# Pairwise outer products with batch normalisation: a rearranged head, and long rows stored in halves with the shortest rows on VectorE

## The chip, the cores and the metric

One core of a Trainium2 chip. The metric is device time in microseconds (us) of one execution; "median" is over the runs of one kernel. All runs told here had the full TensorE clock (granted clock 1.0). Runs of one kernel agree within about 0.7 us, so differences of half a microsecond can be read where a run was repeated five times. The experiments ran in four rounds on four chips; the kernel before, run in each, had medians of 1891.0 to 1891.2 us, so a comparison across rounds carries up to 0.2 us more.

Engines are called PE (TensorE), DVE (VectorE), ACT (ScalarE), POOL (GpSimd) and SP (SyncE, which issues the stores) in the profile.

## The reference

For 1024 samples, 39 fields and 16 components, every pair (row r > column c) gives a 16 x 16 outer product, which is normalised over the batch per pair and weighted:

```python
cross  = xj[:, rows, :, None] * xi[:, cols, None, :]        # (1024, 741, 16, 16)
mean   = jnp.mean(cross, axis=(0, 2, 3), keepdims=True)
var    = jnp.mean(jnp.square(cross - mean), axis=(0, 2, 3), keepdims=True)
normed = (cross - mean) * jax.lax.rsqrt(var + BN_EPS)
normed = normed * gamma[None, :, None, None] + beta[None, :, None, None]
out    = normed[:, :, None, :, :] * W[None, None, :, :, :]  # 777 MB
```

Mean and variance of all 741 pairs follow from small 39 x 39 matrices of moments, so the statistics cost some 30 us; from then on the kernel makes and stores 777 MB.

## The kernel before

A *tile* is one row r (r pairs) of T = 2 of each partition's 8 samples; a tile of a row from 20 to 37 shares one of two slots of a big SBUF buffer with the same samples of the short row 38 - r, which comes right after it. A tile's life:

```python
xs = scale_xi(n)        # POOL: xi * s, s = gamma * rstd per pair
products(n)             # per sample and component i: xs * xj[r, i]; most i on ACT, 4 or 5 of 16 on POOL
finish(n)               # (product + t) * w; DVE one pair of both samples at a time, POOL the row's last 13%
store(n, c0, c1)        # SP: pairs c0..c1; the last piece of a row over 24 is stored sample by sample
```

```python
ONE, TWO = 24, 31
    def bounds(n):
        if n < len(FIRST_PIECES):
            return FIRST_PIECES[n]
        r = tiles[n][0]
        pieces = 1 + (r > ONE) + (r > TWO)          # halves over 24, thirds over 31
        return tuple(q * r // pieces for q in range(pieces + 1))
...
        for n in range(2 * NT // T):                # the head: moments
            square(n)
            emit(raw0, 2)                           # products of tile 0, unscaled, between the squares
            moments(n)
...
        emit(raw_products(1, nc.gpsimd, range(8, 32)), 24)   # tile 1, unscaled too
        emit(raw0, 8)
        nc.scalar.copy(g1, ps_g[0][0:F, 0 : 2 * F + 1])      # the table chain starts here
...
        apply(0)                                    # DVE: gamma and beta into the table of one group of rows
        affine(0)                                   # tiles 0 and 1: scale and shift afterwards
        weigh(0)                                    # DVE: * w, piece by piece, and store
        scale_xi(2)
        affine(1)
        weigh(1)
```

## Time and profile before

| | |
|---|---|
| median | 1891.2 us (1891.1 to 1891.6, 6 runs) |
| output | 777 MB, 414 GB/s over the span |
| first store issued | 41.3 us |
| DVE, ACT, POOL busy | 92, 86, 83% |
| DMA busy | 90% or more in 39 of 40 slices |

One line of the page: the number of packets, each one contiguous run of a partition's row.

```profile
DMA packets 70288, 783.67 MB, mean 415 GB/s; under 512 B 5057, under 2 KB 6209, under 8 KB 15937
```

### The profile page before, as it was taken

The numbers are of one execution on the slowest core, as the hardware profiler recorded it, in microseconds if no ns is written. First come the engines' busy times: TensorE is split into PE (matmuls) and PEld (weight loads), VectorE is DVE, ScalarE is ACT, GpSimd is POOL, SyncE is SP. The second block draws the span as 40 slices with busy tenths as digits, with TensorE's granted clock in tenths as the row PEclk, the third lists the DMA queues.
The fourth block names the chain that finished last, engine by engine and source line by source line (L and its number), as shares of the span: only waits on it lengthen the run. The fifth ranks groups of instructions, "written<-read, shape, count | busy, mean of one in ns | idle before, by whom it ended". The sixth has DMA issues, their size and how long they took to land. (4 is left out here: it accounts for less than half of the span.)

```text
span 1889.3 us, 10288 instructions
## 1 busy us (share of the span) xinstructions
PE 24.5 (1%) x128; PEld 23.1 (1%) x128; DVE 1730.7 (92%) x2612; ACT 1621.3 (86%) x3625; POOL 1574.5 (83%) x1985
## 2 busy tenths in 40 slices
PE   3100000000000000000000000000000000000000
PEld 3100000000000000000000000000000000000000
DVE  7999999998989898989898989899999999999996
ACT  8999989898989898989898989888888888888762
POOL 9798878788888888888888888888888888888972
DMA  4999999999999999999999999999999999999999
GB/s 164 390 418 429 425 427 429 430 424 429 424 425 426 424 424 426 422 425 425 424 425 423 426 423 426 422 422 422 421 421 422 418 415 419 416 419 419 415 419 390
DMA packets 70288, 783.67 MB, mean 415 GB/s; under 512 B 5057, under 2 KB 6209, under 8 KB 15937
## 3 DMA queue, kind: packets, MB, share of 16 engines
q1 hardware_dynamic: 69632, 780.46, 98.3%
q10 hardware_dynamic: 576, 2.56, 0.3%
q14 instruction: 79, 0.64, 0.1%
q8 instruction: 1, 0.02, 0.0%
HBM read 6.00 MB, written 776.99 MB: 414 GB/s over the span
## 5 line engine op out<-in xcount | busy, mean ns | idle before, releaser
L238 DVE SCALAR_TENSOR_TENSOR y_sb<-y_sb,st_sb,w_dve 128x512 f32<-128x512 f32 x2542 | 1678.5, 740 | 131.5 <-issue 128.3
L139 ACT ACTIVATE y_sb<-xs,xj_sb 128x256 f32<-128x256 f32 (+32 forms) x3544 | 1576.4, 539 | 223.5 <-DMA out_dram<-y_sb 171.8
L141 POOL TENSOR_SCALAR y_sb<-xs,xj_sb 128x560 f32<-128x560 f32 (+35 forms) x1256 | 643.2, 536 | 35.1 <-DMA out_dram<-y_sb 32.6
L230 POOL TENSOR_TENSOR y_sb<-y_sb,w_sb 128x1024 f32<-128x1024 f32 (+4 forms) x138 | 442.0, 3203 | 11.5
L159 POOL TENSOR_TENSOR xs<-xi_sb,st_sb 128x576 f32<-128x576 f32 (+37 forms) x150 | 187.8, 1252 | 225.3 <-ACT y_sb L139 217.8
L226 POOL TENSOR_SCALAR y_sb<-y_sb,st_sb 128x512 f32<-128x512 f32 x384 | 259.4, 692 | 12.9 <-ACT y_sb L139 12.9
L204 DVE TENSOR_TENSOR y_sb<-y_sb,w_dve 128x2560 f32<-128x2560 f32 (+5 forms) x8 | 21.0, 2682 | 2.3 <-ACT y_sb L194 2.3
L139 ACT ACTIVATE y_sb<-xi_sb,xj_sb 128x304 f32<-128x304 f32 x40 | 18.7, 534 | 0.1
L414 PE MATMUL ps<-y_sb 39*128 39x38 f32 (+37 forms) x76 | 16.5, 397 | 5.6 <-DVE y_sb L402 5.6
L414 PEld LDWEIGHTS ps<-y_sb 39*128 39x128 f32 x76 | 16.3, 329 | 5.8 <-issue 5.8
L194 ACT ACTIVATE y_sb<-y_sb,st_sb 128x512 f32<-128x512 f32 x20 | 14.2, 797 | 0.0
L196 POOL TENSOR_SCALAR y_sb<-y_sb,st_sb 128x512 f32<-128x512 f32 x18 | 13.5, 771 | 0.3 <-issue 0.3
L141 POOL TENSOR_SCALAR y_sb<-xi_sb,xj_sb 128x304 f32<-128x304 f32 x24 | 11.9, 518 | 0.0
L299 DVE TENSOR_REDUCE y_sb<-y_sb 128x78 f32<-128x1248 f32 x8 | 11.1, 1442 | 0.0
L277 DVE TENSOR_REDUCE y_sb<-xj_sb 128x78 f32<-128x1248 f32 (+1 forms) x5 | 5.9, 1189 | 5.6 <-DMA xj_sb<-in_r_xj_dram 5.6
L293 ACT ACTIVATE y_sb<-y_sb 128x1248 f32<-128x1248 f32 x8 | 9.9, 1243 | 1.3 <-POOL y_sb L283 1.1
L283 POOL TENSOR_TENSOR y_sb<-xj_sb,y_sb 128x1248 f32<-128x1248 f32 x4 | 9.3, 2314 | 1.9 <-ACT y_sb L327 1.9
L283 POOL TENSOR_TENSOR y_sb<-xi_sb,y_sb 128x1248 f32<-128x1248 f32 x4 | 9.3, 2318 | 0.0
L316 PE MATMUL ps<-y_sb 128*39 128x79 f32 x48 | 7.2, 339 | 16.5 <-DVE y_sb L299 16.5
L316 PEld LDWEIGHTS ps<-y_sb 128*39 128x39 f32 x48 | 6.1, 183 | 17.4 <-DVE y_sb L299 9.6
L277 DVE TENSOR_REDUCE y_sb<-xi_sb 128x78 f32<-128x1248 f32 (+1 forms) x5 | 5.9, 1186 | 0.0
L259 POOL TENSOR_SCALAR_AFFINE_SELECT y_sb<-y_sb 39x4992 f32<-39x4992 f32 x1 | 4.6, 4623 | 0.0
(45 smaller groups left out, 16.9 us busy)
## 6 DMA issues: line engine op xcount, KB each, us to landing
out_dram<-y_sb SPq DMA_DIRECT2D x32, 3072.0 KB, 13.7
out_dram<-y_sb SPq DMA_DIRECT2D x28, 2816.0 KB, 15.7
out_dram<-y_sb SPq DMA_DIRECT2D x32, 1664.0 KB, 14.2
out_dram<-y_sb SPq DMA_DIRECT2D x16, 3328.0 KB, 17.2
out_dram<-y_sb SPq DMA_DIRECT2D x30, 1536.0 KB, 15.2
out_dram<-y_sb SPq DMA_DIRECT2D x12, 3840.0 KB, 17.6
out_dram<-y_sb SPq DMA_DIRECT2D x12, 3584.0 KB, 18.1
out_dram<-y_sb SPq DMA_DIRECT2D x22, 1792.0 KB, 17.4
```

What stands on the lines that cost most here:

```text
L139: nc.scalar.activation(y, src, AF.Copy, scale=scale)
L141: engine.tensor_scalar(y, src, scale, 1.0, ALU.mult, ALU.mult)
L159: nc.gpsimd.tensor_tensor(xs, xi_sb[:, t0 : t0 + T, 0:r, :], s_sb[:, :, n0 : n0 + r, :].to_broadcast([P, T, r, E]), ALU.mult,)
L194: nc.scalar.activation(y[:, :, c, :], y[:, :, c, :], AF.Identity, bias=t_c, scale=s_c)
L196: nc.gpsimd.tensor_scalar(y[:, :, c, :], y[:, :, c, :], s_c, t_c, ALU.mult, ALU.add)
L204: nc.vector.tensor_tensor(y[:, :, c0:c1, :], y[:, :, c0:c1, :], w_dve.unsqueeze(1).to_broadcast([P, T, c1 - c0, EE]), ALU.mult,)
L226: nc.gpsimd.tensor_scalar(y[:, :, c, :], y[:, :, c, :], t_sb[:, n0 + c : n0 + c + 1], 1.0, ALU.add, ALU.mult)
L230: nc.gpsimd.tensor_tensor(y[:, :, split:r, :], y[:, :, split:r, :], w_sb.unsqueeze(1).to_broadcast([P, T, r - split, EE]), ALU.mult,)
L238: stt(y[:, :, c, :], y[:, :, c, :], t_sb[:, n0 + c : n0 + c + 1], w_dve.to_broadcast([P, T, EE]), ALU.add, ALU.mult,)
L283: nc.gpsimd.tensor_tensor(devs[n % 7], sources[x][:, t0 : t0 + T], shift[:, x : x + 1, :].unsqueeze(3).to_broadcast([P, T, F, E]), ALU.sub ...
L316: nc.tensor.matmul(acc[0:F, 0 : 2 * F + 1], lhs, fb[:, t], start=t == 0, stop=t == NT - 1)
L414: nc.tensor.matmul(ps[:, :, first[r] - n0 : first[r] - n0 + r], pick[:, r, :], stq[:, :, 0:r], start=True, stop=True,)
```

## The change

Its intent is to send the first store off earlier and to give the late rows larger pieces without starving the stores. The core of the diff, with cuts marked:

```diff
-ONE, TWO = 24, 31
+ONE, LONG = 24, 33
-POOL_I, POOL_I_LONG = 4, 5
+POOL_I, POOL_I_LONG, POOL_I_FIRST = 4, 5, 6      # POOL_I_LONG now for rows over 33, not over 31
+POOL_SHARE, POOL_PAIRS_LONG = 0.13, 8
+SHORT = 4
 ... # head: loads sample by sample, xi before xj, the first xi in two halves;
 ... # the Gram products of x = 1 and x = 0 apart; the square of the table chain on DVE
-        raw1 = raw_products(1, nc.scalar, range(8))          # tile 1 no more prepared before the table
 ...
         apply(0)
-        affine(0)
-        weigh(0)
-        scale_xi(2)
-        affine(1)
-        weigh(1)
-        apply(2)
-        apply(1)
+        apply(1)
+        affine(0, range(0, 11))
+        scale_xi(1)
+        affine(0, range(11, mid))
+        nc.scalar.copy(xj_short, xj_sb[:, :, 1 : SHORT + 1, :])   # for the short rows, in PSUM
+        weigh(0)
+        products(1)                                               # finished sample by sample
 ...
-        pieces = 1 + (r > ONE) + (r > TWO)
+        pieces = 1 + (r > ONE)                                    # halves for all rows over 24
 ...
+        if r <= SHORT:                     # products of rows of up to 4 pairs: three DVE operations
+            nc.vector.tensor_tensor(xs, xi, s_short)              # (arguments cut)
+            for t in range(T):
+                nc.vector.tensor_tensor(view(n)[:, t], xs[:, t], xj_short)
 ...
+        long = r > LONG                    # eight pairs at the end of the first half:
+        for c in range(c0, c1):            # ACT adds t, POOL multiplies by w, in two steps of four
+            nc.scalar.activation(y[:, :, c, :], y[:, :, c, :], AF.Identity, bias=t_c)
+        nc.gpsimd.tensor_tensor(y[:, :, c0:c1, :], y[:, :, c0:c1, :], w_sb, ALU.mult)
```

More of the change, by code (lines that the diff above doesn't have):

```diff
@@ L15 @@
 T = 2
-ONE, TWO = 24, 31
+ONE, LONG = 24, 33
 FIRST_PIECES = (
-    (0, 2, 5, 9, 14, 19), (0, 6, 12, 19), (0, 4, 11, 19), (0, 9, 19), (0, 10, 20), (0, 9, 18), (0, 10, 20), (0, 9, 18)
+    (0, 2, 5, 9, 14, 19), (0, 4, 9, 14, 19), (0, 4, 11, 19), (0, 9, 19), (0, 10, 20), (0, 9, 18), (0, 10, 20), (0, 9, 18)
 )
-POOL_I, POOL_I_LONG = 4, 5
-POOL_SHARE = 0.13
-LOADS = (0, 1, 2, 4, 8)
+POOL_I, POOL_I_LONG, POOL_I_FIRST = 4, 5, 6
+POOL_SHARE, POOL_PAIRS_LONG = 0.13, 8
+LOADS = (1, 2, 3, 4, 8)
+SHORT = 4
 ROW_GROUPS = (
-    (19, 20, 0, None), (15, 19, 1, None), (20, 25, 1, None), (1, 15, 2, 8), (25, 32, 3, 16), (32, 39, 4, 24)
+    (19, 20, 0, None), (15, 19, 1, None), (20, 25, 2, 1), (1, 15, 2, 8), (25, 32, 3, 16), (32, 39, 4, 24)
 )
@@ L71, in tile_pair_outer_batchnorm @@
             slot ^= 1
-    RAW = 2
+    RAW = 1
     cpool = ctx.enter_context(tc.tile_pool(name="cpool", bufs=1))
+    scaled_short = ctx.enter_context(tc.tile_pool(name="scaled_short", bufs=1))
     scaled = ctx.enter_context(tc.tile_pool(name="scaled", bufs=2))
@@ L124, in tile_pair_outer_batchnorm @@
     ps_s, ps_c, ps_g = banks[0], banks[1], banks[2:5]
+    xj_short = ps_c.rearrange("p (t r i) -> p t r i", t=NT, i=E)
     ps_st = banks[5:7] + ps_g
@@ L156, in scale_xi @@
         r, t0, _ = tiles[n]
+        if r <= SHORT:
+            return
         n0 = first[r]
@@ L167, in products @@
     def products(n):
+        r, t0, _ = tiles[n]
+        if r <= SHORT:
+            xs = scaled_short.tile([P, T, r, E], F32, tag="xs_short", name=f"xs_{r}_{t0}")
+            nc.vector.tensor_tensor(
+                xs,
+                xi_sb[:, t0 : t0 + T, 0:r, :],
+                s_short[:, first[r] : first[r] + r]
+                .unsqueeze(1)
+                .unsqueeze(3)
+                .to_broadcast([P, T, r, E]),
+                ALU.mult,
+            )
+            for t in range(T):
+                nc.vector.tensor_tensor(
+                    view(n)[:, t].rearrange("p n (i j) -> p n i j", j=E),
+                    xs[:, t].unsqueeze(2).to_broadcast([P, r, E, E]),
+                    xj_short[:, t0 + t, r - 1 : r, :].unsqueeze(3).to_broadcast([P, r, E, E]),
+                    ALU.mult,
+                )
+            return
         xs = xs_of.pop(n)
-        split = E - (POOL_I_LONG if tiles[n][0] > TWO else POOL_I)
+        split = E - (POOL_I_FIRST if n < 3 else POOL_I_LONG if tiles[n][0] > LONG else POOL_I)
         for t in range(T):
@@ L173, in products, with store @@
                 product(n, nc.scalar if i < split else nc.gpsimd, t, i, xs[:, t])
-    def store(n, c0, c1):
+    def store(n, c0, c1, t_from=0, t_to=T):
         r, t0, _ = tiles[n]
         n0 = first[r]
-        step = 1 if r > ONE and c1 == r else T
-        for t in range(0, T, step):
+        step = 1 if r > ONE and c1 == r else t_to - t_from
+        for t in range(t_from, t_to, step):
             nc.sync.dma_start(
@@ L184, in store, with affine @@
             )
-    def affine(n):
+    def affine(n, pairs):
         r = tiles[n][0]
         y = view(n)
-        for c in range(r):
+        for c in pairs:
             s_c = st_sb[:, 0, first[r] + c : first[r] + c + 1]
@@ L223, in finish @@
         y = view(n)
-        split = r - int(r * POOL_SHARE + 0.5)
-        for c in range(split, r):
-            nc.gpsimd.tensor_scalar(
-                y[:, :, c, :], y[:, :, c, :], t_sb[:, n0 + c : n0 + c + 1], 1.0, ALU.add, ALU.mult
-            )
-        if split < r:
+        long = r > LONG
+        p1 = r // 2 if long else r
+        p0 = p1 - (POOL_PAIRS_LONG if long else int(r * POOL_SHARE + 0.5) if r > SHORT else 0)
+        step = POOL_PAIRS_LONG // 2 if long else r
+        for c0 in range(p0, p1, step):
+            c1 = min(c0 + step, p1)
+            for c in range(c0, c1):
+                t_c = t_sb[:, n0 + c : n0 + c + 1]
+                if long:
+                    nc.scalar.activation(y[:, :, c, :], y[:, :, c, :], AF.Identity, bias=t_c)
+                else:
+                    nc.gpsimd.tensor_scalar(
+                        y[:, :, c, :], y[:, :, c, :], t_c, 1.0, ALU.add, ALU.mult
+                    )
@@ L230, in finish @@
             nc.gpsimd.tensor_tensor(
-                y[:, :, split:r, :],
-                y[:, :, split:r, :],
-                w_sb.unsqueeze(1).to_broadcast([P, T, r - split, EE]),
+                y[:, :, c0:c1, :],
+                y[:, :, c0:c1, :],
+                w_sb.unsqueeze(1).to_broadcast([P, T, c1 - c0, EE]),
                 ALU.mult,
             )
-        for c0, c1 in zip(bounds(n), bounds(n)[1:]):
-            for c in range(c0, min(c1, split)):
-                stt(
-                    y[:, :, c, :],
-                    y[:, :, c, :],
-                    t_sb[:, n0 + c : n0 + c + 1],
-                    w_dve.to_broadcast([P, T, EE]),
-                    ALU.add,
-                    ALU.mult,
-                )
-            store(n, c0, c1)
+        size = 1 if n == RAW else T
@@ new lines, in finish @@
+        for t in range(0, T, size):
+            for c0, c1 in zip(bounds(n), bounds(n)[1:]):
+                for c in [*range(c0, min(c1, p0)), *range(max(c0, p1), c1)]:
+                    stt(
+                        y[:, t : t + size, c, :],
+                        y[:, t : t + size, c, :],
+                        t_sb[:, n0 + c : n0 + c + 1],
+                        w_dve.to_broadcast([P, size, EE]),
+                        ALU.add,
+                        ALU.mult,
+                    )
+                store(n, c0, c1, t, t + size)
@@ L248, in tile_pair_outer_batchnorm @@
     with tc.manual_schedule():
+        nc.gpsimd.memset(ones, 1.0)
+        nc.sync.dma_start(xi_sb[:, 0, 0 : F // 2], xi_v[:, 0, 0 : F // 2])
+        nc.scalar.dma_start(xi_sb[:, 0, F // 2 : F], xi_v[:, 0, F // 2 : F])
+        nc.sync.dma_start(xj_sb[:, 0], xj_v[:, 0])
         for t0, t1 in zip(LOADS, LOADS[1:]):
+            if t1 == NT:
+                nc.scalar.activation(shift_r, ones[0:F, 0:1], AF.Sqrt)
             nc.sync.dma_start(xj_sb[:, t0:t1], xj_v[:, t0:t1])
@@ L255, in tile_pair_outer_batchnorm @@
         nc.sync.dma_start(w_sb[:, 0, :], w.rearrange("o i j -> (o i j)").partition_broadcast(P))
-        nc.gpsimd.memset(ones, 1.0)
         nc.gpsimd.memset(fb[:, :, 2 * F : 2 * F + 1], 1.0 / NB)
@@ L273, in part, with sums @@
             return slice(x * F, (x + 1) * F)
-        def sums(t0, t1):
-            for x in range(2):
+        def sums(t0, t1, xs=(1, 0)):
+            for x in xs:
                 nc.vector.tensor_reduce(
@@ L279, in sums, with step_of @@
                 )
+        def step_of(n):
+            return n // 2 * T, 1 - n % 2
         def deviation(n):
-            t0, x = n // 2 * T, n % 2
+            t0, x = step_of(n)
             nc.gpsimd.tensor_tensor(
@@ L290, in square @@
         def square(n):
-            scale = 0.25 / NB**0.5 if n % 2 else 0.25
+            _, x = step_of(n)
+            scale = 0.25 / NB**0.5 if x else 0.25
             nc.scalar.activation(devs[n % 7], devs[n % 7], AF.Square, scale=scale)
         def moments(n):
-            t0, x = n // 2 * T, n % 2
+            t0, x = step_of(n)
             to = fb if x else fa
-            at = slice(F, 2 * F)
-            nc.vector.tensor_reduce(to[:, t0 : t0 + T, at], devs[n % 7], AX.X, ALU.add)
-        def means(n):
-            t0, x = n // 2 * T, n % 2
-            to = fb if x else fa
-            stt(
-                to[:, t0 : t0 + T, 0:F],
-                total[:, t0 : t0 + T, part(x)],
-                1.0 / (E * NB) if x else 1.0 / E,
-                ps_u[:, x : x + 1, :].to_broadcast([P, T, F]),
-                ALU.mult,
-                ALU.subtract,
-            )
@@ L313, in gram, with means @@
-        def gram(t0):
+            nc.vector.tensor_reduce(
+                to[:, t0 : t0 + T, F : 2 * F], devs[n % 7], AX.X, ALU.add
+            )
+        def means(t0, t1):
+            for x, to in enumerate((fa, fb)):
+                stt(
+                    to[:, t0:t1, 0:F],
+                    total[:, t0:t1, part(x)],
+                    1.0 / (E * NB) if x else 1.0 / E,
+                    ps_u[:, x : x + 1, :].to_broadcast([P, t1 - t0, F]),
+                    ALU.mult,
+                    ALU.subtract,
+                )
@@ L314, in gram @@
+        def gram(n):
+            t0, x = step_of(n)
             for t in range(t0, t0 + T):
-                for acc, lhs in zip(ps_g, (fa[:, t, 0:F], fa[:, t, F : 2 * F], ones[:, 0:F])):
+                terms = ((0, fa[:, t, 0:F]), (2, ones[:, 0:F])) if x else ((1, fa[:, t, F : 2 * F]),)
+                for acc, lhs in terms:
                     nc.tensor.matmul(
-                        acc[0:F, 0 : 2 * F + 1], lhs, fb[:, t], start=t == 0, stop=t == NT - 1
+                        ps_g[acc][0:F, 0 : 2 * F + 1], lhs, fb[:, t], start=t == 0, stop=t == NT - 1
@@ L318, in gram @@
                     )
-        raw0 = raw_products(0, nc.scalar, range(32))
-        raw1 = raw_products(1, nc.scalar, range(8))
-        nc.scalar.activation(shift_r, ones[0:F, 0:1], AF.Sqrt)
-        sums(0, 1)
-        nc.tensor.matmul(ps_s[:, 0 : 2 * F], ones, total[:, 0], start=True, stop=True)
-        nc.tensor.matmul(ps_c[0:F, 0:1], total[:, 0, 0:F], ones[:, 0:1], start=True, stop=True)
-        nc.scalar.activation(
-            shift.rearrange("p x f -> p (x f)"), ps_s[:, 0 : 2 * F], AF.Copy, scale=k_s
-        )
+        raw0 = raw_products(0, nc.scalar, range(24))
@@ new lines, in tile_pair_outer_batchnorm @@
+        raw0_pool = raw_products(0, nc.gpsimd, range(24, 32))
+        ps_shift = (ps_g[0][:, 0:F], ps_s[:, 0:F])
+        for x in (1, 0):
+            sums(0, 1, (x,))
+            nc.tensor.matmul(ps_shift[x], ones, total[:, 0, part(x)], start=True, stop=True)
+        nc.tensor.matmul(ps_c[0:F, 0:1], total[:, 0, 0:F], ones[:, 0:1], start=True, stop=True)
+        ps_u = ps_s[:, 2 * F : 4 * F].rearrange("p (x f) -> p x f", x=2)
+        nc.scalar.activation(shift[:, 1], ps_shift[1], AF.Copy, scale=k_s)
@@ L330, in tile_pair_outer_batchnorm @@
+        nc.scalar.activation(ps_u[:, 1], shift[:, 1], AF.Copy, scale=1.0 / NB)
+        nc.scalar.activation(shift[:, 0], ps_shift[0], AF.Copy, scale=k_s)
+        nc.scalar.copy(ps_u[:, 0], shift[:, 0])
         nc.scalar.activation(shift_r, ps_c[0:F, 0:1], AF.Copy, scale=k_s)
-        ps_u = ps_s[:, 2 * F : 4 * F].rearrange("p (x f) -> p x f", x=2)
-        nc.scalar.copy(ps_u[:, 0], shift[:, 0])
-        nc.scalar.activation(ps_u[:, 1], shift[:, 1], AF.Copy, scale=1.0 / NB)
         def cell(n):
@@ L343, in tile_pair_outer_batchnorm @@
         sums(1, 2)
-        means(0)
-        means(1)
-        sums(2, 4)
-        means(2)
-        means(3)
+        means(0, 2)
+        sums(2, 3)
+        sums(3, 4)
+        means(2, 4)
         for n in range(7):
@@ L355, in tile_pair_outer_batchnorm @@
             moments(n)
+            gram(n)
             if n == 0:
                 deviation(7)
-            if n % 2 == 1:
-                gram(n // 2 * T)
-            if n in (1, 3):
-                sums(n + 3, n + 5)
-                means(n + 3)
-                means(n + 4)
-        emit(raw_products(1, nc.gpsimd, range(8, 32)), 24)
+            if n == 1:
+                sums(4, 8)
+                means(4, 8)
+        emit(raw0_pool, 8)
         nc.scalar.copy(w_dve, w_sb)
-        emit(raw0, 8)
         nc.scalar.copy(g1, ps_g[0][0:F, 0 : 2 * F + 1])
+        emit(raw0, 1)
         nc.scalar.copy(e_aa, ps_g[1][0:F, 2 * F : 2 * F + 1])
-        emit(raw0, 5)
+        emit(raw0, 4)
         e_ab, e_abb, e_a = g1[:, 0:F], g1[:, F : 2 * F], g1[:, 2 * F : 2 * F + 1]
@@ L380, in tile_pair_outer_batchnorm @@
         stt(k, p_b, u, e_ab, ALU.mult, ALU.add)
-        stt(q2, e_ab, u, p_aab, ALU.mult, ALU.add)
+        stt(p_q1, p_bb, u, e_abb, ALU.mult, ALU.add)
         stt(k, p_v, e_a, k, ALU.mult, ALU.add)
-        stt(q2, p_v_half, e_aa, q2, ALU.mult, ALU.add)
-        stt(p_q1, p_bb, u, e_abb, ALU.mult, ALU.add)
-        stt(p_q2, q2, 2.0, p_v, ALU.mult, ALU.mult)
         nc.vector.tensor_add(q1, p_q1, e_abb)
         stt(p_mean, p_v, u, k, ALU.mult, ALU.add)
-        nc.scalar.activation(p_kk, k, AF.Square)
+        nc.vector.tensor_mul(p_kk, k, k)
+        stt(q2, e_ab, u, p_aab, ALU.mult, ALU.add)
         stt(q1, q1, u, p_aabb, ALU.mult, ALU.add)
+        stt(q2, p_v_half, e_aa, q2, ALU.mult, ALU.add)
+        nc.vector.tensor_sub(q1, q1, p_kk)
+        stt(p_q2, q2, 2.0, p_v, ALU.mult, ALU.mult)
         nc.vector.tensor_add(q1, q1, p_q2)
-        nc.vector.tensor_sub(q1, q1, p_kk)
         nc.vector.tensor_scalar(p_var, q1, 0.0, BN_EPS, ALU.max, ALU.add)
@@ L396, in tile_pair_outer_batchnorm @@
         nc.scalar.activation(rstd, inv, AF.Sqrt)
-        emit(raw1, 8)
         nc.vector.tensor_mul(p_newton, p_var, rstd)
@@ L421, in tile_pair_outer_batchnorm @@
             spread_of.append((ps, n0, n1))
+            if r0 == 1:
+                s_short = ps[:, 0]
         def apply(group):
@@ L425, in apply @@
             nc.vector.tensor_mul(ps[:, 1], ps[:, 1], st_sb[:, 0, n0:n1])
-            nc.vector.tensor_mul(st_sb[:, 0, n0:n1], ps[:, 0], st_sb[:, 0, n0:n1])
+            nc.vector.tensor_mul(ps[:, 0], ps[:, 0], st_sb[:, 0, n0:n1])
+            nc.vector.tensor_copy(st_sb[:, 0, n0:n1], ps[:, 0])
             nc.vector.tensor_add(st_sb[:, 1, n0:n1], ps[:, 1], st_sb[:, 1, n0:n1])
         apply(0)
-        affine(0)
+        apply(1)
[3 more added lines that the diff above has]
+        nc.scalar.copy(xj_short, xj_sb[:, :, 1 : SHORT + 1, :])
         weigh(0)
+        products(1)
         scale_xi(2)
-        affine(1)
-        weigh(1)
-        apply(2)
-        apply(1)
         for n in range(1, len(tiles)):
-            if n == 1:
-                products(2)
-                scale_xi(3)
-                continue
             if n + 2 < len(tiles):
```

## The prediction

> **What bounds the kernel now.** I read the page first (busy shares and the row of DMA digits), then the table of stretches, then the chain of waits, then the head in order of time.
>
> ```profile
> PE 24.5 (1%) x128; PEld 23.1 (1%) x128; DVE 1730.7 (92%) x2612; ACT 1621.3 (86%) x3625; POOL 1574.5 (83%) x1985
> DMA  4999999999999999999999999999999999999999
> HBM read 6.00 MB, written 776.99 MB: 414 GB/s over the span
> ```
>
> Three engines look nearly full, but the DMA row is full in every slice but the first. The output alone is 777 MB; no engine can matter except by starving the stores. The stretches say how full the DMA engines are and what they move (last two numbers: DMA share, GB/s):
>
> ```profile
> 44.00:66.00 22.00, 9.22 (x43) 9.01 (x43) 20.46 (x16) 22.00 (x44) 15.90 (x24) 1.00 1.00 403
> 66.00:86.00 20.00, 0.00 (x0) 0.00 (x0) 20.00 (x32) 20.00 (x46) 16.42 (x23) 1.00 0.88 360
> ...
> 300.00:500.00 200.00, 0.00 (x0) 0.00 (x0) 188.15 (x288) 182.63 (x412) 167.14 (x215) 1.00 1.00 427
> 1000.00:1300.00 300.00, 0.00 (x0) 0.00 (x0) 275.34 (x418) 261.23 (x587) 252.54 (x330) 1.00 1.01 423
> 1300.00:1490.00 190.00, 0.00 (x0) 0.00 (x0) 172.90 (x263) 158.58 (x367) 165.61 (x215) 1.00 1.01 421
> 1490.00:1740.00 250.00, 0.00 (x0) 0.00 (x0) 226.49 (x343) 207.60 (x490) 214.73 (x269) 1.00 1.00 417
> 1740.00:1876.00 136.00, 0.00 (x0) 0.00 (x0) 124.30 (x189) 81.18 (x134) 99.98 (x102) 1.00 0.99 415
> ```
>
> So there are three places where time can be had: the head before the first store, one hole at 66 to 86 us (0.12 of 20 us = 2.4 us), and the late rows, where full DMA engines move 415 to 417 GB/s instead of 427. The rate falls with the length of the stored rows. By the trace's packet records a packet of 12288 bytes takes 466 ns, one of 18432 takes 692, one of 24576 takes 920: about 0.037 ns per byte and some 13 ns per packet.
>
> In the late rows (about 37 pairs to a tile) the chain of waits alternates:
>
> ```profile
> 1724.86 5.94 DVE y_sb L238 x9
> ...
> 1730.85 11.62 DMA out_dram<-y_sb
> ...
> 1742.58 3.88 ACT y_sb L139 x6
> ```
>
> The last third's store is issued at 1730.85, lands at 1742.48, and ScalarE then refills that slot; the same point one turn earlier is 1694.49, so 48.1 us for two tiles, 24.05 each. Bytes alone, from the packet durations, need 23.8. The ring slot, products, VectorE, store, landing is as long as the transfer: its holes in the records are only 0.2 to 0.5 us per long tile, 5 us from 1490 us to 1876 us.
>
> **The head.** The end of the statistics and the table chain in order of time (VectorE):
>
> ```profile
> 23.83 5.52 DVE L299 TENSOR_REDUCE y_sb<-y_sb 128x78 f32<-128x1248 f32 x4
> 32.00 0.25 DVE L380 SCALAR_TENSOR_TENSOR y_sb<-ps,y_sb 39x39 f32<-39x39 f32 x1 [2.65 <-ACT y_sb L372]
> ...
> 34.35 0.19 DVE L391 TENSOR_TENSOR y_sb<-y_sb,ps 39x39 f32<-39x39 f32 x1 [0.18 <-ACT ps L388]
> ...
> 36.42 0.19 DVE L402 SCALAR_TENSOR_TENSOR y_sb<-ps,y_sb 39x39 f32<-39x39 f32 x1
> ...
> 40.03 1.22 DVE L204 TENSOR_TENSOR y_sb<-y_sb,w_dve 128x1024 f32<-128x1024 f32 x1 [2.13 <-ACT y_sb L194]
> ```
>
> VectorE waits 2.65 us for ScalarE to copy the Gram matrix (which it does after eight raw products), and 2.13 us before the first weighting because ScalarE is in its last eight raw products of tile 1. The first store is issued at 41.27.
>
> **What the Trainium skill says.** "DMA: Bandwidth & Descriptors", Where 436 GB/s comes from: 16 ports give 435 GB/s at most. The best stretch here, 427, is near it, and I take the body as immovable. The same page, Why a DMA increments its semaphore by 16 and not by 1: engines finish independently and only the full count means landed. The trace agrees: of the third issued at 1717.77 most engines had drained the packets by 1726, but it landed at 1731.5; some engine lags by up to 5 us, and the ring waits for that one. "SBUF — State Buffer", Who interferes with whom: a VectorE instruction with two SBUF inputs contends with a GpSimd instruction that reads SBUF. The change gives the new VectorE products a PSUM operand, so I charge nothing for it; nothing in the trace before tests it. "GPSIMD Engine Reference", 3.1 Elementwise: 2048 float32 of tensor_tensor in 4497 ns; the trace has 4520 ns for 128x2048, and I use the trace's.
>
> **The change part by part.**
>
> 1. Table chain. The x = 1 Gram terms go out one moment earlier, so the copy of the Gram matrix no longer waits for the last moment; the last GpSimd and ScalarE work is out of the way. That removes the 2.65 wait. One more VectorE operation (about 0.2) replaces the ScalarE square and its 0.18 wait. From the last moment to the last table operation: before, 36.61 - 29.35 = 7.26; after, about 13 small operations 2.8, reciprocal 0.43, root 0.27, five operations 1.15: 4.65. Gain 2.6.
>
> 2. From the table to the first store. ScalarE is free, so the affine starts at about +1.65 and has ended by +2.4 us. But VectorE now does two applies before the weighting, the second of which waits for five rows of spreading matmuls (16.46 us for 38 rows is 0.43 each, so +2.3), then four operations of 0.22: weighting at +3.3, before 40.03 - 36.61 = 3.4. Gain 0.1.
>
> 3. Loads and statistics. Halves of the first xi should land about 0.7 us before today's 4.9, and deviations can start about 1 us before today's 7.63. But VectorE is the limit of this stage: it works from 4.93 to 29.35 with 0.9 us idle, and its work stays about 23.4. Eleven loads are asked for where eight were, and the last ones (samples 4 to 8) wait for a landing of the first before they are issued. They landed at 15 and 16 us; VectorE will want them at about 14.5, and 14.2 us of reductions follow: last moment at 29 to 30.2. Loss 0.4, between a gain of 0.6 and a loss of 0.9. First store at 41.3 - 2.6 - 0.1 + 0.4 = 39.0.
>
> 4. After the first store. Tile 1 is no longer prepared before the table exists. ScalarE must scale it afterwards: affine 10 x 0.71, a copy 0.7, then 20 products of 0.44 (8.8 us) for each of tiles 1 and 2. GpSimd's two pairs of tile 1 come last, at about +23.3 us after the table; tile 2's VectorE work then starts near +29.3, where today it starts at 63.96 - 36.61 = 27.35. I estimate holes of 5 us instead of the 3 in the early records: loss 2, uncertain by 2 either way.
>
> 5. Halves for rows 32 to 38 instead of thirds. Seven rows, four tiles, 256 packets fewer each: 7168 x 13 ns / 16 engines = 5.8 us; one more piece in tile 1 gives back 0.2. Gain 5.5. This lies on the path, since the DMA engines are full.
>
> 6. The ring in rows over 33. Twenty-four ScalarE products of 0.2 us and eight of GpSimd's per short tile go away; VectorE takes three operations (about 1 to 2.7 us) but loses four pairs of 0.66. For 37 pairs VectorE needs about 21 of 23.5 us. The first store of a tile, however, now needs ScalarE's four biases (2.9 us) and GpSimd's two multiplications (4.5 each): 11.9 us after the products instead of 7.9 for a third. Against that, the last quarter that frees the slot is issued as a half tile's sample, so its first sample has 5.9 instead of 4 us of transfer behind it. Ring for 37 pairs: products 15.2, 13.1 to the first packet, 11.1 + 5.9 of transfer, 0.3: 45.5 plus the lag of the slowest engine, against 2 x 23.5 = 47. For 38 it is 46.3 plus lag against 46.7. So rows 34 to 36 gain up to the 0.25 us per tile of holes, and row 38 may lose as much as 1 us per tile. I book 2 of the 5 us as gained.
>
> Sum: -2.3 (1 to 3), +2 (4), -5.5 (5), -2 (6) = -7.8 us, so about 1883.5.
>
> **The rivals.** (a) The ring becomes the bound in rows 37 and 38: a half must be whole before anything goes out, and it hangs on ScalarE and GpSimd in turn. Against it is the slack above; for it the lag of up to 5 us. With 1 us lost in each of 8 to 16 tiles the result is 1892 to 1899 less the packets' 5.5: 1886 to 1893. (b) The head's gain is swallowed by holes in tiles 1 to 3, because work was moved from before the table to after it; then 1886. (c) The late rows reach the 424 GB/s of 18 KB packets with no holes: 386 us at 416.5 become 379, and with the head's full 4 us: 1878. (d) VectorE becomes the bound; 90% busy in the late rows and falling, I don't expect it.
>
> **Range and chances.** The packets' gain is nearly certain (5 to 6); head and early holes are 0 plus or minus 3; the ring -5 to +6. Predicted 1883.5, 8 in 10 between 1877 and 1889. Leaving 2% (1853 or 1929) would take 38 us, more than all holes together: 1% each way.
>
> **What would show it.** First store between 38 and 40 us, no wait of 2.65 before the table chain, the last moment at 29 to 30. Holes between 55 and 90 us; if they are under 3 us, step 4 is wrong. About 7,000 fewer packets on the output queue, and the late stretches at 421 GB/s or more; if they stay at 417 with shares below 1.00, rival (a) is true and ScalarE's waits on GpSimd or on the landing will have grown. If the span falls by over 14 us, the lagging engine was a cost that I took to be fixed.

## The result

The changed kernel takes 1883.9 us (1883.8 to 1884.3, 6 runs), 7.3 us less than before; the ratio is 0.9962, with a 95% interval of 0.9949 to 0.9974. Ratios are the mean time of one kernel's fast runs over that of the other's of the same rounds, so not quite the ratio of the medians that are quoted. The forecast was 1883.5.

The page of the changed kernel, four lines:

```profile
PE 26.0 (1%) x130; PEld 23.3 (1%) x130; DVE 1724.6 (92%) x2636; ACT 1641.5 (87%) x3408; POOL 1524.5 (81%) x1736
DMA  4999999999999999999999999999999999999999
DMA packets 63434, 783.63 MB, mean 416 GB/s; under 512 B 4736, under 2 KB 6144, under 8 KB 16256
HBM read 6.00 MB, written 776.99 MB: 416 GB/s over the span
```

ScalarE has 217 instructions fewer and still 20 us more work: eight biases of 512 columns a tile in rows over 33 (100 us in all) in place of 24 small products (85 us), and two products more a tile in rows 32 and 33 (10 us), less what it saves in the head. There are 6854 packets fewer for the same bytes.

The stretches of the changed kernel, in the order of those shown of before (last numbers: DMA share, GB/s):

```profile
44.00:66.00 22.00, 6.79 (x32) 6.58 (x31) 20.93 (x44) 22.00 (x51) 20.42 (x32) 1.00 0.96 384
66.00:86.00 20.00, 0.00 (x0) 0.00 (x0) 20.00 (x32) 20.00 (x46) 18.62 (x26) 1.00 0.84 344
...
300.00:500.00 200.00, 0.00 (x0) 0.00 (x0) 188.20 (x288) 182.63 (x413) 167.48 (x215) 1.00 1.00 427
...
1000.00:1300.00 300.00, 0.00 (x0) 0.00 (x0) 275.22 (x417) 267.84 (x598) 245.92 (x320) 1.00 1.00 423
1300.00:1490.00 190.00, 0.00 (x0) 0.00 (x0) 177.18 (x265) 163.12 (x315) 153.23 (x154) 1.00 1.00 423
1490.00:1740.00 250.00, 0.00 (x0) 0.00 (x0) 228.35 (x351) 208.02 (x316) 194.78 (x135) 1.00 1.00 422
1740.00:1876.00 136.00, 0.00 (x0) 0.00 (x0) 107.11 (x166) 96.49 (x143) 89.24 (x62) 1.00 0.99 422
```

The late stretches moved from 417 and 415 to 422 GB/s at the same DMA share: the same busy engines move more. The two early stretches got worse, 0.96 and 0.84 instead of 1.00 and 0.88. The body is unchanged.

The head of the changed kernel on VectorE, in order of time, cut to the same places as before:

```profile
21.61 8.25 DVE L348 TENSOR_REDUCE y_sb<-y_sb 128x78 f32<-128x1248 f32 x6
29.95 0.25 DVE L428 SCALAR_TENSOR_TENSOR y_sb<-ps,y_sb 39x39 f32<-39x39 f32 x1
...
33.99 0.19 DVE L449 SCALAR_TENSOR_TENSOR y_sb<-ps,y_sb 39x39 f32<-39x39 f32 x1
...
37.50 10.54 DVE L231 TENSOR_TENSOR y_sb<-y_sb,w_dve 128x1024 f32<-128x1024 f32 x5
...
63.44 11.94 DVE L277 SCALAR_TENSOR_TENSOR y_sb<-y_sb,st_sb,w_dve 128x512 f32<-128x512 f32 x18 [1.00 <-POOL y_sb L146]
```

The last moment ends at 29.86 instead of 29.35, the table is ready at 34.18 instead of 36.61, and the first weighting starts at 37.50 instead of 40.03; the first store is issued at 38.74 instead of 41.27. The wait of 2.65 us ahead of the chain is gone.

A *hole* is time in which DMA engines move nothing, added up over the 16 engines and divided by 16; its size below is from the packet records. Where the 7.3 us came from is best read from the same records: the time at which all bytes up to the end of a given tile or row had been written, less that time in the kernel before. (Two kernels of the experiments below stand beside it.)

| bytes written up to the end of | changed | head alone | late rows alone |
|---|---|---|---|
| tile 0 (56 us) | -2.9 | -3.0 | -0.2 |
| tile 2 (82 us) | -0.5 | -1.2 | +0.3 |
| tile 3 (94 us) | -0.3 | -0.9 | +0.4 |
| row 30 (1126 us) | -0.4 | -1.1 | +0.3 |
| row 33 (1409 us) | -0.1 | -1.1 | +0.5 |
| row 35 (1600 us) | -2.4 | -1.0 | -1.6 |
| row 37 (1791 us) | -4.3 | -1.0 | -3.3 |
| end (1888 us) | -6.9 | -1.0 | -5.7 |

A head that is 2.5 us shorter is worth 0.3 us four tiles later. Nothing happens for 1300 us. The rest is earned in rows 34 to 38, 2.6 us of it in row 38 alone.

### The profile page after: what moved, and what is told of

The parts are those of the page before. It is cut to its first block, busy times and chain, and to the rows that moved or that the text cites. A ratio compares the mean times of both kernels' runs of the same rounds, so it can differ in the third digit from the quotient of the medians.

```text
span 1882.2 us, 9655 instructions
## 1 busy us (share of the span) xinstructions
PE 26.0 (1%) x130; PEld 23.3 (1%) x130; DVE 1724.6 (92%) x2636; ACT 1641.5 (87%) x3408; POOL 1524.5 (81%) x1736
## 5 line engine op out<-in xcount | busy, mean ns | idle before, releaser
L277 DVE SCALAR_TENSOR_TENSOR y_sb<-y_sb,st_sb,w_dve 128x512 f32<-128x512 f32 (+1 forms) x2516 | 1654.0, 737 | 130.4 <-issue 117.5
L144 ACT ACTIVATE y_sb<-xs,xj_sb 128x288 f32<-128x288 f32 (+21 forms) x3192 | 1509.9, 567 | 194.5 <-DMA out_dram<-y_sb 163.8
L146 POOL TENSOR_SCALAR y_sb<-xs,xj_sb 128x384 f32<-128x384 f32 (+27 forms) x1128 | 607.0, 565 | 43.7 <-DMA out_dram<-y_sb 28.0
L266 POOL TENSOR_TENSOR y_sb<-y_sb,w_sb 128x2048 f32<-128x2048 f32 (+3 forms) x155 | 511.8, 3308 | 104.1 <-ACT y_sb L261 94.5
L166 POOL TENSOR_TENSOR xs<-xi_sb,st_sb 128x640 f32<-128x640 f32 (+33 forms) x135 | 184.3, 1365 | 175.6 <-ACT y_sb L144 170.8
L263 POOL TENSOR_SCALAR y_sb<-y_sb,st_sb 128x512 f32<-128x512 f32 x286 | 193.9, 695 | 0.1
L261 ACT ACTIVATE y_sb<-y_sb,st_sb 128x512 f32<-128x512 f32 x160 | 100.2, 708 | 1.9
L189 DVE TENSOR_TENSOR y_sb<-xs,ps 128x1024 f32<-128x1024 f32 (+3 forms) x32 | 24.8, 817 | 0.6
L223 POOL TENSOR_SCALAR y_sb<-y_sb,st_sb 128x512 f32<-128x512 f32 x9 | 6.8, 775 | 7.1 <-issue 7.1
L144 ACT ACTIVATE y_sb<-xi_sb,xj_sb 128x304 f32<-128x304 f32 x24 | 11.6, 534 | 0.0
L231 DVE TENSOR_TENSOR y_sb<-y_sb,w_dve 128x2560 f32<-128x2560 f32 (+3 forms) x5 | 10.5, 2174 | 0.0
L221 ACT ACTIVATE y_sb<-y_sb,st_sb 128x512 f32<-128x512 f32 x10 | 7.2, 802 | 2.8 <-DVE st_sb L477 2.8
```

The costliest lines, as they stand in the source:

```text
L144: nc.scalar.activation(y, src, AF.Copy, scale=scale)
L146: engine.tensor_scalar(y, src, scale, 1.0, ALU.mult, ALU.mult)
L166: nc.gpsimd.tensor_tensor(xs, xi_sb[:, t0 : t0 + T, 0:r, :], s_sb[:, :, n0 : n0 + r, :].to_broadcast([P, T, r, E]), ALU.mult,)
L189: nc.vector.tensor_tensor(view(n)[:, t].rearrange("p n (i j) -> p n i j", j=E), xs[:, t].unsqueeze(2).to_broadcast([P, r, E, E]), xj_short ...
L261: nc.scalar.activation(y[:, :, c, :], y[:, :, c, :], AF.Identity, bias=t_c)
L263: nc.gpsimd.tensor_scalar(y[:, :, c, :], y[:, :, c, :], t_c, 1.0, ALU.add, ALU.mult)
```

## The experiments

The theory: the stores bound the kernel; the late rows gain by larger packets, and the head's gain is lost in holes before tile 3. The rivals: the ring (products, VectorE, store, landing) and not the packets sets the late rows; or the parts do not add.

### 1. The two halves of the change, each alone

*Late rows alone*: the head of before (with `raw1` and `affine(1)`), and from the changed kernel `products`, `bounds`, `finish`, `store` and the PSUM copies that the short rows need. *Head alone*: the changed kernel with

```diff
-ONE, LONG = 24, 33
+ONE, LONG, TWO = 24, 39, 31
-SHORT = 4
+SHORT = 0                                    # and the copy to xj_short taken out
-        pieces = 1 + (r > ONE)
+        pieces = 1 + (r > ONE) + (r > TWO)
-        ... POOL_I_LONG if tiles[n][0] > LONG
+        ... POOL_I_LONG if tiles[n][0] > TWO
```

> The head of the kernel before, with the changed kernel's late rows alone (halves for rows over 24, rows of up to 4 pairs on VectorE, eight pairs of rows over 33 on ScalarE and GpSimd). Additive theory: between the two traces the changed kernel is 0.3 to 0.4 us ahead from tile 3 up to row 30, and gains the rest, about 6.6 us, from there to the end. So this run should be 6.4 to 7.1 us faster than the kernel before: 1884.1 to 1884.8 us. Rival: the shorter head is worth its whole 2.5 us at the end and the late rows give only 4.8; then 1886.4 us.

> The changed kernel's head (loads, chain, tile 1 made after the table), with the late rows of the kernel before (thirds for rows over 31, short rows on ScalarE and GpSimd, GpSimd's share at the row's end). Additive theory: the first store goes out at 38.7 us instead of 41.3, but the holes before tile 3 eat 2.2 of these 2.5 us: 0.2 to 0.6 us faster than before, 1890.6 to 1891.0 us. Rival: 2.5 us faster, 1888.7 us.

Measured, five runs each: late rows alone 1885.24 us (-5.95), head alone 1889.85 us (-1.34); the kernel before beside them 1891.19. The sum, -7.29, is the whole change (-7.31): the parts add, within the noise. But neither size is what was expected: the head is worth 1.3 and not 0.4, the late rows 6.0 and not 6.7. The table above shows why. The late rows alone are 0.35 us *behind* at tile 3, before any late row: their copy of four xj rows into PSUM stands in ScalarE's way in the head. Without that copy the head leads by 0.9 us. (The late rows alone also have the changed kernel's `apply`, with one VectorE copy more for each group of rows, 0.2 to 0.3 us; that was not tested by itself.)

### 2. The copy, moved to where ScalarE has time

```diff
-        nc.scalar.copy(xj_short, xj_sb[:, :, 1 : SHORT + 1, :])     # between affine(0) and products(1)
...
+            if n == 60:
+                nc.scalar.copy(xj_short, xj_sb[:, :, 1 : SHORT + 1, :])
```

> The changed kernel with one edit: ScalarE's copy of the four xj rows into PSUM (0.58 us, between the affine of tile 0 and the products of tile 1) moved to the middle of the run, where it is first needed 600 us later. The head alone had gained 1.3 us, with this copy 0.4 less than that at tile 3, and the late rows alone showed tile 3 0.35 us late. Theory: ScalarE's products set the holes at 57 and 66 us, so all of 0.58 us comes back: 1883.2 to 1883.5. Rival: VectorE or GpSimd sets them and nothing comes back: 1883.9.

1883.36 us, 0.5 less than the changed kernel, as expected. In the packet records 0.7 to 0.8 us are back from tile 1 to row 35, of which the last rows keep 0.5. The copy itself, in the changed kernel's trace:

```profile
35.85 7.16 ACT L221 ACTIVATE y_sb<-y_sb,st_sb 128x512 f32<-128x512 f32 x10 [2.81 <-DVE st_sb L477]
42.91 0.58 ACT L485 COPY ps<-xj_sb 128x512 f32<-128x512 f32 x1
```

It is 0.58 us between two things that the next store waits for, and it is first used in row 34, after 1400 us.

### 3. GpSimd's pairs of tile 1

```diff
+        if n == RAW:
+            p0 = p1                       # tile 1: all 19 pairs on VectorE
```

> The changed kernel with one edit: GpSimd takes no pairs of tile 1, VectorE takes all 19. Theory of the swallowed head: the hole at 57 us (1.1 us) ends when GpSimd's two pairs of tile 1 are multiplied at 57.5 us, and tile 2's products by GpSimd start only then. Without them that hole goes, GpSimd starts tile 2 about 3.7 us earlier, VectorE pays 4 more operations of 0.36 us, tile 2 starts 0.4 to 1 us earlier: 1 to 1.8 us faster than the changed kernel, 1882.1 to 1882.9 us. Rival: the holes are set by ScalarE's 72 products in a row from 43.4 to 75.3 us, and nothing moves: 1883.9 us.

1884.38 us: 0.5 *slower* than the changed kernel. A miss. GpSimd was indeed done 3.7 us earlier, and the hole at 57 us (1.1 us) went. But 0.6 us came at 60 to 64 us, and the next hole, at 64 to 68 us, grew from 1.2 to 2.2 us. VectorE in that run:

```profile
48.13 14.97 DVE L279 SCALAR_TENSOR_TENSOR y_sb<-y_sb,st_sb,w_dve 128x256 f32<-128x256 f32 x38
...
64.01 26.42 DVE L279 SCALAR_TENSOR_TENSOR y_sb<-y_sb,st_sb,w_dve 128x512 f32<-128x512 f32 x40
```

Tile 2 starts at 64.01 instead of 63.44: the four operations more that VectorE took over are the difference. They cost more than the 1.00 us for which VectorE had waited there for GpSimd. There is no idle time ahead of it now, and it is GpSimd that waits for VectorE (4.4 us, at 64 us). In the changed kernel the two end within 1 us of each other here, and taking work from one to give it to the other moves the hole.

### 4. Halves without the rest, and thirds with the rest

```diff
 # halves_only: the kernel before
-        pieces = 1 + (r > ONE) + (r > TWO)
+        pieces = 1 + (r > ONE)
 # thirds: the changed kernel
-        pieces = 1 + (r > ONE)
+        pieces = 1 + (r > ONE) + (r > 31)
```

> The kernel before with one edit: rows over 31 in halves instead of thirds. 7168 packets fewer, 5.8 us less DMA work. Packet theory: that is the gain, 1885.4 us. Ring theory: with ScalarE still making the short rows and VectorE alone making a half of 16 to 19 pairs (10.6 to 12.5 us instead of 7.9) before anything can be stored, the slot's ring gets longer than the transfer, holes of 0.5 to 1 us per long tile open and give back 3 to 8 us: 1888 to 1893 us, with a DMA share below 1.00 after 1300 us and the packet count still 7168 lower. I expect 1888.

> The changed kernel with one edit: rows over 31 stored in thirds again. 7168 packets come back. If packets are what the late rows gained by, this is 5 to 6 us slower than the changed kernel, 1889 to 1890 us, with the late stretches back at 417 to 421 GB/s. Rival, from halves alone having given 4.4 us of the 6: the ring gets shorter again (a third of 12 pairs is ready 4 us earlier), so holes of 1.8 us at 1200 to 1420 us go and only 3 to 4 us are lost: 1887 to 1888. I expect 1888.5.

Halves put alone into the kernel before: 1886.75 us, -4.44. I had expected the ring to eat more (1888). Thirds put back into the changed kernel: 1889.78 us, 5.9 us slower, the upper end of what was expected. The late stretches of the changed kernel, then of the one with thirds:

```profile
1420.00:1700.00 280.00, 0.00 (x0) 0.00 (x0) 260.46 (x395) 232.82 (x356) 219.09 (x156) 1.00 1.00 423
1700.00:1860.00 160.00, 0.00 (x0) 0.00 (x0) 136.94 (x212) 128.90 (x192) 119.08 (x80) 1.00 1.00 421
```

```profile
1420.00:1700.00 280.00, 0.00 (x0) 0.00 (x0) 256.16 (x388) 228.57 (x352) 213.09 (x150) 1.00 1.01 420
1700.00:1860.00 160.00, 0.00 (x0) 0.00 (x0) 135.41 (x212) 134.78 (x201) 121.03 (x86) 1.00 1.00 418
```

Full DMA engines in both, 3 GB/s less with the smaller packets. That is the packets' effect with no wait in it, some 3 us in these 440 us. The total DMA work of the changed kernel's stores, summed over the packet records and divided by 16 engines, is 1838.6 us, that of before 1845.0; the difference, 6.4 us, is close to all that the late rows gave.

The 5.9 us of this run are not packets alone, though. In the last 3 us before its last packet ends the DMA engines are idle for 2.67 us on average (from 1885.3 us on a single packet at a time is in flight), against 0.12 us in the changed kernel and 1.10 us in the kernel before: one engine ends later than the others. On the other hand, the thirds have 2.0 us less of holes from 1200 us on. Without both, some 5.3 us are left for the packets; halves alone (4.44 us, with 1.9 us more of holes and 1.0 us less at the end) leave the same 5.3. These are estimates that take holes and the late end to add up.

The ring's part is small but real. It shows at 1219 us, where row 32 begins: changed kernel, and the one with thirds.

```profile
1217.00:1221.00 4.00, 0.00 (x0) 0.00 (x0) 4.00 (x7) 4.00 (x8) 3.92 (x11) 1.00 0.74 311
```

```profile
1217.00:1221.00 4.00, 0.00 (x0) 0.00 (x0) 4.00 (x7) 4.00 (x7) 3.92 (x11) 1.00 1.01 424
```

The first half of row 32 is 16 pairs, 10.6 us of VectorE, where a third was 10 pairs; its store is issued at 1218.88 instead of 1214.49 in the kernel before. Between 1200 and 1420 us the changed kernel has holes of 1.8 us, where before and with thirds there are none. The halves alone have 1.7 us there, so it is the halves that open them and not the work that was moved.

### 5. What the short rows and the eight pairs are for

```diff
 # short_act: the changed kernel
-SHORT = 4
+SHORT = 0                                     # and the copy to xj_short taken out
 # no_split: the changed kernel
-        long = r > LONG
+        long = False                          # POOL takes 13% at the row's end, ACT no biases
```

> The changed kernel with one edit: rows of up to 4 pairs again on ScalarE and GpSimd, ScalarE keeping its eight biases for each row over 33. ScalarE per long and short tile: 22 products of 0.69 (15.2), eight biases 5.0, 24 short products 4.9: 25 us where the transfer takes 23.5. If the short rows were moved to make room on ScalarE, 16 tiles lose 1.2 to 1.6 us each: 1900 to 1908 us. Rival: moving them saved only instructions that were hidden: 1883.3 to 1884 (the copy of 0.6 us in the head is saved as well).

> The changed kernel with one edit: in rows over 33 GpSimd takes its 13% at the row's end as before, and ScalarE no biases. VectorE per long and short tile at row 34: 30 x 0.66 + 2.9 for the short products + 4 x 0.66 = 25.3 us, at row 35 24.0, row 36 23.3, against a transfer of 23.5: rows 34 and 35 become bound by VectorE and lose some 6 to 8 us in all: 1890 to 1892 us. Rival: the backlog and the shorter wait for the first half (11.2 us by VectorE alone instead of 11.9) cover it: 1884 to 1885.

Both as expected: 1903.29 us (19.4 slower than the changed kernel) and 1890.83 us (7.0 slower). One stretch of each, short rows on ScalarE first, then without the eight pairs (DVE, ACT, POOL busy are the third to fifth of the values):

```profile
1420.00:1700.00 280.00, 0.00 (x0) 0.00 (x0) 221.92 (x336) 278.98 (x607) 239.50 (x250) 1.00 0.95 401
```

```profile
1420.00:1700.00 280.00, 0.00 (x0) 0.00 (x0) 279.23 (x424) 167.01 (x252) 207.10 (x195) 1.00 0.98 412
```

In the one ScalarE is busy 278.98 of 280 us, in the other VectorE 279.23. Each of the two moves alone overloads the engine that it moves work to; only together do they leave all three below the transfer (260, 233 and 219 of 280 us in the changed kernel). What the pair of them brings is the 1.5 us by which late rows alone (-5.95) beat halves alone (-4.44).

### 6. Variants meant to be faster

All of them start from the late copy (1883.36 us). *Early*: the second apply out of the first weighting's way, the third into VectorE's idle time, 5 instead of 6 products of tile 2 on GpSimd, and more pieces in tiles 2 to 4:

```diff
-    ..., (0, 4, 11, 19), (0, 9, 19), (0, 10, 20), (0, 9, 18), (0, 10, 20), (0, 9, 18)
+    ..., (0, 4, 8, 13, 19), (0, 5, 10, 14, 19), (0, 5, 11, 20), (0, 8, 18), (0, 9, 20), (0, 9, 18)
-    ... (15, 19, 1, None), (20, 25, 2, 1), ...
+    ... (15, 19, 1, 2), (20, 25, 2, None), ...
-        apply(1)                                  # ahead of affine(0); apply(2) now after weigh(0)
```

*Late*: a shorter ring in rows 32, 33, 37 and 38:

```diff
-        ... POOL_I_LONG if tiles[n][0] > LONG
+        ... POOL_I_LONG if tiles[n][0] > 31
+        pairs_long = 6 if r > 36 else POOL_PAIRS_LONG
```

> The variant with the late copy (1883.36 us), and the waits of tiles 0 to 4 that its trace shows taken out: the apply of rows 15 to 18 no longer stands between the table and the first weighting (first store 0.7 us earlier, about 37.9), the apply of rows 20 to 24 lies in VectorE's idle time before tile 1, GpSimd makes 5 instead of 6 of 16 products of tile 2 (tile 2 starts at 61.8 instead of 62.7), and tiles 2 to 6 are stored in more or other pieces. Holes before 100 us fall from 4.9 to about 2.7 us, four pieces more cost 1024 packets, 0.8 us: 1.5 to 2.2 us faster, 1881.2 to 1881.9 us. Rival: VectorE at 0.66 us a pair is slower than the transfer at 0.62, so each hole that closes opens again one tile later and the packets cost extra: 1883.4 to 1884.

> The variant with the late copy, and the ring shortened where its trace shows holes: 10 instead of 8 products of rows 32 and 33 on GpSimd (ScalarE is 1.25 us per tile shorter), and 6 instead of 8 pairs of rows 37 and 38 on ScalarE and GpSimd, so that their first half is ready 8.7 instead of 11.6 us after the products and VectorE, at 21 to 22 us, still stays under 23.2. If the ring makes the holes of 1.7 us at 1200 to 1420 us and of 2.1 after 1700 us, half of them go, and the tail is up to 1 us shorter: 1.5 to 3 us faster, 1880.4 to 1881.9. Rival: the slowest DMA engine sets these rows and the others' holes are only its shadow: 1883.2 to 1883.5.

> Both of these edits together. If the kernel is bound by the stores throughout, the two gains add: 3 to 5 us under the variant with the late copy, 1878.5 to 1880.4 us. If the early gain is lost again in the late rows, where the ring and not the transfer sets the pace, less than the sum.

1884.43, 1883.73 and 1884.52 us: all three misses, each slower than its base by 0.4 to 1.2 us (0.5 to 1.3 against the kernel before of the same round, since the base ran in another). Both edits together are no better than the early one alone. The misses teach more than the hits.

*Early* led its base by 2.2 us at tile 3 and 1.9 at 117 us, and was 0.5 behind at 188 us. All of it went at one place: 138 to 142 us. There tile 8 is stored, the first one that goes out whole. The stretch in the kernel before, the changed one, and the early variant:

```profile
138.00:142.00 4.00, 0.00 (x0) 0.00 (x0) 3.97 (x9) 4.00 (x10) 3.83 (x5) 1.00 0.86 359
```

```profile
138.00:142.00 4.00, 0.00 (x0) 0.00 (x0) 3.93 (x9) 4.00 (x11) 3.92 (x6) 1.00 0.92 386
```

```profile
138.00:142.00 4.00, 0.00 (x0) 0.00 (x0) 3.93 (x9) 4.00 (x10) 3.92 (x5) 1.00 0.28 116
```

VectorE has no pause from the start of tile 2 to here in any of them, and its next work after tile 8 starts at 140.99, 140.46 and 139.85 us. Whatever the stores had gained before, they wait for that.

*Late* issued the first halves of the last rows 3 us earlier, and they landed no earlier. Issues from 1800 to 1870 us of the changed kernel and of the late variant (size, and median us from issue to landing):

```profile
out_dram<-y_sb SPq DMA_DIRECT2D x3, 4864.0 KB, 13.8
```

```profile
out_dram<-y_sb SPq DMA_DIRECT2D x3, 4864.0 KB, 16.9
```

The 3 us went into the queue. The ring had made holes all the same: two stretches at the end of the base with the late copy, then of the late variant.

```profile
1700.00:1875.00 175.00, 0.00 (x0) 0.00 (x0) 141.69 (x219) 128.20 (x191) 118.74 (x79) 1.00 0.99 421
1875.00:1880.00 5.00, 0.00 (x0) 0.00 (x0) 0.00 (x0) 0.00 (x0) 0.00 (x0) 1.00 1.02 436
```

```profile
1700.00:1875.00 175.00, 0.00 (x0) 0.00 (x0) 151.62 (x234) 119.74 (x177) 103.58 (x79) 1.00 1.01 426
1875.00:1880.00 5.00, 0.00 (x0) 0.00 (x0) 0.00 (x0) 0.00 (x0) 0.00 (x0) 1.00 0.64 272
```

Up to 1875 us the holes are gone, 2.1 us in the base and none here. But in the base 16 packets are in flight until 0.2 us before the end. Here most engines are done at 1878.4 us, and from 1879.0 to 1880.9 us a single packet at a time is in flight. The last engine ends 0.4 us later than in the base (the last store lands at 1881.3 instead of 1880.8 us), however early the others are done. That fits the rival: the slowest DMA engine sets these rows, and the others' holes are time in which they wait for it. Why one engine is slower, no run shows. In rows 32 and 33 the edit changed nothing (1.8 us of holes, 1.7 in the base).

### 7. Tiles 8 to 12 in halves

Added to the early variant:

```diff
     ... (0, 9, 20), (0, 9, 18),
+    (0, 10, 20), (0, 9, 18), (0, 10, 20), (0, 9, 18), (0, 10, 21)
```

> The early variant (1884.43 us) with one edit more: tiles 8 to 12, which are stored whole there, go out in two halves. In every kernel so far the stores have a hole at 138 to 142 us, at tile 8, the first tile stored whole: 0.6 us in the kernel before, the changed one and the one with the late copy, 2.9 us in the early variant, and it ends at 141.9, 141.6, 140.9 and 141.4 us, the order of their end times but for the late rows. VectorE has worked without a pause since tile 1 and its end of tile 8 sets the pace anew; what was gained before is lost there. With halves the wait there is up to 6 us shorter: that hole goes, the 1.9 to 2.2 us by which the early variant leads at 117 us stay, less 1280 packets (1.0 us). Then about 1882.0 to 1882.9 us, 1 us below the variant with the late copy. Rival: VectorE is short of the stores in each of the tiles 8 to 14, the hole reopens at tile 13 or later: 1884.4 to 1885.4.

1883.08 us (1882.7 to 1883.3), 1.35 under the early variant, but short of the 1882.0 to 1882.9 that were expected: a miss in size. The same stretch:

```profile
138.00:142.00 4.00, 0.00 (x0) 0.00 (x0) 3.93 (x10) 4.00 (x10) 3.92 (x5) 1.00 0.99 411
```

The hole is gone, and the lead over the base is still 2.0 us at the end of row 20. It is 1.4 after row 21 and 1.1 from row 23 to row 30, and 0.3 at the end. (The 2304 packets more of both edits are 2.1 us of DMA work, but all except 256 of them are stored before the end of row 20, so they don't explain what is lost after it.) It is the fastest kernel, 0.8 us under the changed one, which is 0.04%; the 0.3 us under its base, run in another round, are hardly more than the noise. Why the late rows do not keep the early lead is open: the slowest DMA engine, as in the late variant, would do it, but no run shows it here.

## Why the prediction was right

The time was right to 0.4 us, but partly because two errors cancelled. Step by step:

1. *Table chain, gain 2.6.* Measured 2.9 (from the last moment to the last table operation 7.26 before, 4.32 after). Right.
2. *To the first store, gain 0.1.* Weighting starts 3.32 us after the table, as the prediction's 3.3. Right, and for the reason given: the second apply waits (1.00 us) for the spreading matmuls, which copy the table to all 128 partitions.
3. *Loads and statistics, loss 0.4.* The last moment came 0.5 later, with the wait for the last load (1.60 us ahead of the reductions) that was expected. First store at 38.74, forecast 39.0.
4. *Holes after the first store, loss 2.* The size was right for the changed kernel: from the first packet to 100 us there are 3.5 us of holes before and 5.4 after, and tile 2's VectorE work starts 29.26 us after the table, forecast 29.3. VectorE's wait ahead of it (1.00 us) is for GpSimd, whose two pairs of tile 1 were named; but that wait is not what the loss hangs on: with the pairs given to VectorE (experiment 3) it is gone and the kernel is slower. ScalarE's copy was counted as 0.7 us inside the step, but it belongs to the late rows, and moved away it gave 0.5 back. And VectorE, which was held not to become a bound in the late rows, has no idle time from tile 2 to tile 8: it reaches the end of tile 8 only 0.5 us earlier than before, whatever went before. So the head by itself was worth 1.3 us, where steps 1 to 4 had summed to 0.3.
5. *Packets, gain 5.5.* 6992 packets fewer on the stores' queue (6912 of them stores), 6.4 us less DMA work, 5.9 us when undone by itself, of which some 5.3 are the packets' (experiment 4). Right.
6. *The ring, gain 2.* This is the step that failed. The late rows as a whole gave 6.0 us, or 6.5 without the copy's cost, where steps 5 and 6 summed to 7.5. The ring was booked as a gain and was about zero. Rows 34 to 38 did lose part of their holes (5.0 before, 3.1 after, from 1420 to 1880 us), the 2 us that were booked, and row 38, where a loss of up to 1 us a tile was feared, gained 2.6 us, some 1.0 of them because all engines now end together. But rows 32 and 33, to which the step gave no thought, opened 1.8 us of new ones. Rival (a), the half that must be whole before anything goes out, was looked for in rows 37 and 38 and came in rows 32 and 33, where VectorE alone makes the half. And in the last rows holes turned out to be no measure of the time: the late variant filled them all (2.1 us from 1700 to 1875 us) and ended later, since one engine did.

Rival (b), the head's gain swallowed, was half true; (c), late rows at 424 GB/s without holes, was nearly the truth for the rate (422 to 423) but not for the head; (d) was false for late rows as shipped and true as soon as the eight pairs were given back to VectorE; with the short rows given back, ScalarE became the bound.

Two sums among the rivals do not add up, without touching the 1883.5: (a) takes the packets' 5.5 off a second time (1883.5 and 8 to 16 us are 1892 to 1899 with them in), and 7 and 4 us off 1891.2, as in (c), are 1880 and not 1878.

## What to carry to other kernels

When stores bound a kernel, time gained before the first store lasts only as far as the next tile whose store must wait for a full piece; look for that tile along the whole run before shortening the head, and cut *its* piece. Fewer, longer packets are worth about their count times the fixed cost (here some 5.3 us of 5.8) even when each store is already several megabytes, provided that the first piece is ready in time. Where holes are an average over 16 DMA engines, look also at when the last engine ends: filling the others' holes (2.1 us in the late variant) gained nothing. A move of work from engine A to B and another from B to C can each be a loss alone and still be needed together.

## What the Trainium skill lacked or had wrong

- "DMA: Bandwidth & Descriptors", Rules for kernel authors, asks for at least 1 MiB per DMA for the highest rate. The stores of rows over 31 were 1.4 MB and more with thirds too; packets of 10 to 13 KB instead of 16 to 19 KB cost 5.9 us in some 670 us of late rows, of which about 5.3 are the packets' (420 and 418 against 423 and 421 GB/s with full DMA engines). The page's Bandwidth section gives about 10.5 ns a packet, for a 4 KB load of 64 packets issued from GpSimd; by the packet records a store here costs about 13 ns a packet beyond its bytes.
- The same page, Why a DMA increments its semaphore by 16 and not by 1, says that engines finish independently but not by how much. Here the slowest lagged by up to 5 us (a third issued at 1717.77 us, mostly drained by 1726, landed at 1731.5), a fifth of the transfer of a long tile, and in the late variant the last one ended 2.5 us after most others.
- "SBUF — State Buffer", Summary: rules for kernel authors, advises some 358 GB/s as the estimate for transfers between HBM and SBUF. On the one core that this kernel uses, stores ran at 421 to 427 GB/s for most of the run. The point is against this line only.
- No page says what VectorE's `scalar_tensor_tensor` costs. In an unbroken stream it is 0.66 us for 512 columns (19.84 us for 30) and 0.39 us for 256 (13.41 us for 34): finishing a tile sample by sample costs 0.13 us more a pair, which mattered where VectorE was the bound.
